# A decoder layer on one NeuronCore: the row transposes and masked sums of the last head groups, made at 32 columns in second PSUM banks

## Chip, cores and metric

The kernel runs on one core of one Trainium2 chip. The metric is device time in microseconds (us) for one launch. Before the change the median of three runs is 803.79 us (803.73 to 803.90).

## What is computed

A pre-LayerNorm decoder layer for 4 sequences of 512 tokens with 512 features and 16 heads of 32, all in fp32:

```python
x = x + self_attention(layernorm(x))        # wq, wk, wv, wo with biases; causal, masked scores -inf
x = x + cross_attention(layernorm(x), ctx)  # q = layernorm(x), k = v = ctx; causal, masked scores -10000
h = layernorm(x)
x = x + relu(h @ Wup.T) @ Wdown.T + sum(softmax(top2(h @ Wgate.T))) * (h @ Wexp)
```

For each head, attention is `softmax(where(causal, q k^T / sqrt(32), masked)) v`. In the cross attention the mask is the finite number -10000, so a masked column still weighs exp(-10000 - row maximum); the kernel carries these weights as a count of the masked columns and a sum of the values behind the diagonal.

## The kernel before

**Stages.** Sequences b = 0 to 3 follow each other. Each has a self attention (its names end in s0 to s3) and a cross attention (c0 to c3), and each attention has two halves. `with_maxima` makes the row maxima of all scores, and mixes in ("fills" with) matmuls of other stages: projections, and the feed-forward network of the sequence before. `attend` makes the scores a second time, exponentiates them and multiplies by the values. Output projection, LayerNorms and feed-forward stand between.

**Groups and units.** The 16 heads form four groups g = 0 to 3 of four heads, whose 4 x 32 features fill 128 partitions. Keys come in four blocks j of 128. `attend` walks ten units n = 0 to 9 of (g, j): (0,0) | (0,3),(0,1) | (0,2),(1,2) | (1,0) | (1,3),(1,1) | (2,0) | (2,3),(2,1) | (2,2),(3,2) | (3,0) | (3,3),(3,1). In each step n it records `scores` of unit n, and from n = 2 on `values` of the unit two before. Scores lie transposed: keys on partitions, queries on columns, two heads in a PSUM pair, so that one unit fills two pairs.

**Row maxima into the scores.** The split (-maximum in three bf16 pieces, `parts[g % 2]`) is transposed by `rows(g)` into PSUM and copied to `mrow[g]`, and a matmul with `onesb` (L416) adds it to the scores before the exponential (L439). So `rows(2)` must be done ahead of unit 5 and `rows(3)` ahead of unit 7. `masked_sums(g)` (L371) is, for cross attention alone, a matmul of `mrow[g]` with a block matrix `same`; `masked(g)` (L377) exponentiates it (`ct_c`) and puts it into the sums.

**Sums of a softmax row.** For the groups in `added` (self 0, 1, 2; cross 0, 2) the exponentials of all key blocks are added up elementwise on DVE (`add_up`, L552) into the tile `sum_` and summed over keys at the end by `summed(g)` (L556-564), a quad of matmuls with a matrix of ones (L558). For other groups the values' matmuls are followed by matmuls with ones (L482). In the self attention `shares` (L466) puts `summed(0)` into the second bank of `pv[1]`, at group 1's first unit, and `summed(1)` into that of `pv[2]`. In the cross attention `summed(g)` goes to the second bank of `pv[g]`. In cross, DVE's `divide`, and POOL's `scale` (L574) follow for the group before. The tile of sums is taken from a pool with one buffer for each tag:

```python
self.sums[g] = act.tile(                     # L428, for units (g, 0) of added groups
    [P, 2, 2, S], F32,
    tag="v" if self.cross else ("ck_t", "beh_t")[g % 2], name=f"sum_{name}")
```

So in the self attention `sum_` of groups 0 and 2 lie in the same buffer.

**PSUM** is one pool `ps` of four buffers, each a pair of banks of 512 fp32 columns (L63-67). Two of them usually go to score pairs, and `pv[g]` holds a pair from its group's first value to its division. Transposes of rows and masked sums take a pair of their own.

**Order.** The instructions of PE, DVE, ACT and POOL stand in the order in which the program is written (`manual_schedule`, L1000; `BY_HAND`, L17). The tile framework adds buffers and the waits between engines. Queued behind a waiting instruction is thus all that is written later for its engine. POOL runs `affine_select` (L447), which sets masked exponentials to zero, and the multiplications of `scale`.

**Around the change, before.** `with_maxima` returns `late`, which says at which step of `attend` rows are made. Its default is {3: 3}: in the self attention both rows(2) and rows(3) are made at n = 3 (one pair `mt_s_both`, eight transposes, two ACT copies); in the cross attention rows(2) is made at the end of `with_maxima`, and rows(3) together with masked_sums(2) at n = 3 (`mt_c_both`). All self stages and c0 to c2 take this path. c3, whose fill has fewer than 20 matmul steps, has {3: 2, 5: 3}. masked_sums(3) of all cross stages is made at n = 7 in a pair of its own (`mb_c`), ahead of that step's values.

Of the kernel before, what the change touches and what calls it, by code (L numbers as in the profile page):

```python
# [18 lines left out]
P = 128  # L19
# [7 lines left out]
def decoder_layer(  # L27
# [21 lines left out]
    nc = tc.nc  # L49
    B, S, D = x.shape  # L50
    NH = 16
    HD = D // NH
    NT = S // P
    NC = D // P
# [10 lines left out]
    def pair(name):  # L65

        return ps.tile([P, 2, S], F32, tag="ps", name=name)
# [198 lines left out]
    class Attention:  # L266
# [82 lines left out]
            nc.vector.tensor_copy(pt[:, :, :, 1], rest)  # L349
            nc.vector.tensor_tensor(pt[:, :, :, 2], rest, pt[:, :, :, 1], ALU.subtract)  # L350

        def rows(self, g, both=None, half=0):


            if both is None:
                tp = ps.tile([P, NT, P], BF16, tag="ps", name=f"mt_{self.name}_{g}")
            else:
                bank = both[:, 0, :].bitcast(BF16)
                tp = bank[:, half * S : (half + 1) * S].rearrange("p (i q) -> p i q", q=P)
            for i in range(NT):  # L360
                nc.tensor.transpose(tp[:, i, :], parts[g % 2][:, i, :], identb)
            self.mrow[g] = work.tile(
                [P, S], BF16, tag="mrow", name=f"mrow_{self.name}_{g}", bufs=4
            )

            def copy(engine=nc.vector.tensor_copy):
                engine(self.mrow[g], tp.rearrange("p i q -> p (i q)"))

            return [copy]

        def masked_sums(self, g, both=None):  # L371

            bc = (pair(f"mb_{self.name}_{g}") if both is None else both)[:, 1, :]
            nc.tensor.matmul(bc, lhsT=same, rhs=self.mrow[g], start=True, stop=True)
            return g, bc

        def masked(self, g, bc):  # L377
# [88 lines left out]
        def shares(self, g, blocks):  # L466

            js = {j for j, *_ in blocks}
            first = js == {0} if g % 2 == 0 else js == {2}
            last = js == {2} if g % 2 == 0 else 1 in js  # L470
            if first:
                self.pv[g] = pair(f"pv_{self.name}_{g}")
            pv = self.pv[g]
            for u in range(1 if g in self.added else 2):
                if u and g == self.joined and (0 in js or 2 in js):
                    if 0 in js:
                        self.joint_sums(pv, blocks[0][2])
                    continue
                for n, (j, c, pts) in enumerate(blocks):
                    for r in range(HG):  # L480
                        h = g * HG + r
                        nc.tensor.matmul(  # L482
                            pv[r * HD : (r + 1) * HD, u, j * P :],
                            lhsT=ones if u else self.v[:, j, h * HD : (h + 1) * HD],
                            rhs=pts[r // 2][:, r % 2, c : c + S - j * P],
                            start=first,
                            stop=last and n == len(blocks) - 1,
                            skip_group_check=True,
                        )
            if self.cross:  # L490


                if (first if g == 1 else js == {0}) and g - 1 in self.added:
                    self.summed(g - 1, self.pv[g - 1])
                    self.divide(g - 1)
                elif js == {0} and g > 0:
                    self.scale(g - 1)
                if 1 in js and g == NC - 1:
                    self.scale(g - 1)
                if last and g not in self.added:  # L500
                    self.divide(g)
                    if g == NC - 1:
                        self.scale(g)
                return
            if first and g == 0:
                self.out = act.tile([P, NC, S], F32, tag="o_t", name=f"oT_{self.name}")
            if (first if g in self.added else js == {0}) and g - 1 in self.added:
                self.sum_in = pv if g in self.added else pair(f"ls_{self.name}")
                self.summed(g - 1, self.sum_in)
            if js == {0} and g - 2 in self.added:  # L510
                self.scale(g - 2)
            if 1 in js and g - 1 in self.added and g not in self.added:
                self.spread(g - 1, self.sum_in)
                self.scale(g - 1)
            if last and g in self.added:
                nc.scalar.copy(self.out[:, g, :], pv[:, 0, :])
                if g > 0:
                    self.spread(g - 1, pv)
            elif last:
                num, den = pv[:, 0, :], pv[:, 1, :]  # L520
                nc.vector.tensor_tensor(
                    self.out[:, g, :], num, self.inverse(g, den), ALU.mult
                )
# [381 lines left out]
    def with_maxima(steps, a, first=0, norms=()):  # L905


        norms = list(norms)
        run(steps[:first])
        fill = matmuls(steps[first:])  # L910
        total = sum(1 if step.__name__ in ("share", "gate") else NC for step in steps[first:])

        units = []
        for g in range(0, NC, 2):
            units += [[(g, 1), (g + 1, 1)]]
            units += [u for k in (g, g + 1) for u in ([(k, 2), (k, 0)], [(k, NT - 1)])]

        lead = 2 if first else 0
        for _ in range(lead):
            next(fill)  # L920
        done, due, jobs, late = lead, float(lead), [], {3: NC - 1}
        todo = []
        for n, pieces in enumerate(units):
            new = a.maxima(pieces)
            if todo:
                todo.pop()(nc.gpsimd)
            if norms and n % 2 == 0:
                new.append(norms.pop(0))
            due += (total - lead) / len(units)

            count = round(due) - done
            for k in range(count):
                next(fill, None)
                done += 1
                if k == min(1, count - 1) and n in (5, 7):
                    jobs = a.rows((n - 5) // 2) + jobs
                if k == min(1, count - 1) and a.cross and n in (6, 8):
                    todo.append(a.masked(*a.masked_sums((n - 6) // 2)))
                if n == len(units) - 1 and k == count - (2 if count > 4 else 1):
                    if total >= 2 * len(units):  # L940
                        if a.cross:
                            a.rows(2)[0](nc.scalar.copy)
                    else:
                        late = {3: 2, 5: NC - 1}
                run(jobs[:1])
                jobs = jobs[1:]
            run(jobs)
            jobs = new
        for _ in fill:
            pass  # L950
        run(jobs)
        return late

    def attend(a, late):


        units = []
# [5 lines left out]
        def values():  # L963
            made = waiting.pop(0)
            a.values(made)

            if len(made) > 1 and made[0][1] == 2:
                held.append(made[1:])
            elif waiting and waiting[0][0][1] > 0:
                if made[0][1] == 0 and held:  # L970
                    a.add_up(held.pop())
                a.add_up(waiting[0] if waiting[0][0][1] == 3 else waiting[0][:1])
                if waiting[0][0][1] == 2 and waiting[0][1][0] == a.joined:
                    a.join(waiting[0][1], waiting[1][0])

        for n, pieces in enumerate(units):
            waiting.append(a.scores(pieces))
            if n in late:
                two = a.cross and late[n] == NC - 1
                together = not a.cross and len(late) == 1  # L980
                both = pair(f"mt_{a.name}_both") if two or together else None
                copies = a.rows(2, both, 1) if together else []
                copies += a.rows(late[n], both)

                more = [a.masked_sums(2, both)] if two else []
                for copy in copies:
                    copy(nc.scalar.copy)
                todo.extend(a.masked(*each) for each in more)
            if a.cross and n == 7:
                todo.append(a.masked(*a.masked_sums(3)))  # L990
            if n in (4 if a.joined is None else 6, 6, 9) and todo:
                todo.pop(0)()
            if n in (3, 4) and put_off:
                put_off.pop(0)()
            if len(waiting) > 2:
                values()
        while waiting:
            values()

# [112 lines left out]
```

## Time and profile before

| | before |
| --- | --- |
| median of the runs | 803.79 us |
| span of the profiled execution | 803.68 us |
| mean granted clock of TensorE (PE) | 0.998 |
| PE busy | 794.0 us, 99% |
| DVE busy | 565.9 us, 70% |
| ACT busy | 395.2 us, 49% |
| POOL busy | 339.6 us, 42% |
| self attention s1, `attend` | 249.9 to 280.1 us of the span |
| cross attention c0, `attend` | 157.4 to 189.2 us of the span |

PE runs matmuls, DVE, ACT and POOL elementwise work. A group of the profile is named by the line of code, the engine, the operation, output and inputs, and its shape. In PE's rows 128\*32 means that 128 rows and 32 columns of the array are used, so that four such matmuls can stand side by side; 32\*128 means that 32 rows are used. "Busy" counts a group from its first to its last matmul, and the ends of matmuls are modelled. An entry such as [0.33 <-PE sc_s L416] says that an engine was idle for 0.33 us in front of this work, and whose end it waited for.

### The profile page before, as it was taken

The numbers are of one execution on the slowest core, as the hardware profiler recorded it, in microseconds if no ns is written. First come the engines' busy times: TensorE is split into PE (matmuls) and PEld (weight loads), VectorE is DVE, ScalarE is ACT, GpSimd is POOL, SyncE is SP. The second block draws the span as 40 slices with busy tenths as digits, with TensorE's granted clock in tenths as the row PEclk, the third lists the DMA queues.
The fourth block names the chain that finished last, engine by engine and source line by source line (L and its number), as shares of the span: only waits on it lengthen the run. The fifth ranks groups of instructions, "written<-read, shape, count | busy, mean of one in ns | idle before, by whom it ended". The sixth has DMA issues, their size and how long they took to land.

```text
span 803.7 us, 13927 instructions
## 1 busy us (share of the span) xinstructions
PE 794.0 (99%) x5588; PEld 378.9 (47%) x5592; DVE 565.9 (70%) x963; ACT 395.2 (49%) x448; POOL 339.6 (42%) x523
## 2 busy tenths in 40 slices
PE   8999999999999999999999999999999999999998
PEld 6444454444444454444544455444444444444544
DVE  2378855889679854678867786588959766988512
ACT  2457516871456615567055742687156833674110
POOL 3434612564234732257332482256423652475100
PEclk9999999999999999999999999999999999999999
DMA  9710000001010000021100000000102000000101
GB/s 301 275 28 1 2 1 1 2 27 54 1 27 2 2 0 1 2 78 55 53 14 14 1 2 0 1 1 2 53 28 80 2 1 1 1 2 1 53 1 52
DMA packets 15282, 24.51 MB, mean 30 GB/s; under 512 B 2033, under 2 KB 5361, under 8 KB 15217
## 3 DMA queue, kind: packets, MB, share of 16 engines
q1 hardware_dynamic: 14496, 22.96, 8.6%
q8 instruction: 44, 0.72, 0.4%
q10 hardware_dynamic: 720, 0.66, 0.2%
q14 instruction: 22, 0.17, 0.1%
HBM read 19.42 MB, written 4.19 MB: 29 GB/s over the span
## 4 chain that ended last, share of the span: by engine, by line
PE 95%; ACT 2%; issue 1%; DMA 1%; DVE 0%; ACTq 0%
PE pm_qk L241 14%; PE pm_d L229 7%; PE pm_u L241 7%; PE pm_v L229 7%; PE pm_o L725 7%; PE pm_e L229 7%; PE pv_c L482 6%; PE pv_s L482 6%; PE sm_c L293 6%; PE sm_s L293 6%; PE sc_s L405 5%; PE sc_c L405 5%; PE sc_s L416 1%; PE sc_c L416 1%; PE tp_a L255 1%
## 5 line engine op out<-in xcount | busy, mean ns | idle before, releaser
L324 DVE TENSOR_REDUCE nm_s<-s_s 128x2 f32<-128x1024 f32 (+3 forms) x128 | 96.9, 810 | 34.7 <-POOL s_s L312 34.7
L324 DVE TENSOR_REDUCE nm_c<-s_c 128x2 f32<-128x1024 f32 (+3 forms) x128 | 95.8, 810 | 31.0 <-POOL s_c L312 31.0
L304 ACT COPY s_s<-sm_s 128x1024 f32<-128x1024 f32 x80 | 77.1, 1015 | 70.7 <-PE sm_s L293 36.7
L304 ACT COPY s_c<-sm_c 128x1024 f32<-128x1024 f32 x80 | 77.1, 1016 | 35.9 <-PE sm_c L293 16.2
L312 POOL TENSOR_SCALAR_AFFINE_SELECT s_c<-s_c 128x512 f32<-128x512 f32 (+1 forms) x80 | 43.9, 550 | 100.4 <-ACT s_c L304 100.4
L312 POOL TENSOR_SCALAR_AFFINE_SELECT s_s<-s_s 128x512 f32<-128x512 f32 (+1 forms) x80 | 43.8, 551 | 94.4 <-ACT s_s L304 94.4
L552 DVE TENSOR_TENSOR sum_s<-sum_s,pt_s 128x256 f32<-128x256 f32 (+2 forms) x72 | 59.9, 897 | 15.4 <-PE pv_s L482 15.4
L439 ACT ACTIVATE pt_c<-sc_c 128x1024 f32<-128x1024 f32 x64 | 61.7, 1031 | 18.1 <-PE sc_c L416 10.1
L447 POOL TENSOR_SCALAR_AFFINE_SELECT pt_c<-pt_c 128x512 f32<-128x512 f32 (+1 forms) x64 | 52.9, 833 | 20.7 <-ACT pt_c L439 20.2
L229 PE MATMUL pm_d<-wdown_sb,hT 128*128 128x512 f32 x128 | 61.5, 611 | 0.0
L241 PE MATMUL pm_qk<-xnT,wk_sb 128*128 128x512 f32 x128 | 61.0, 606 | 0.0
L241 PE MATMUL pm_u<-fT,wup_sb 128*128 128x512 f32 x128 | 59.3, 605 | 0.0
L439 ACT ACTIVATE pt_s<-sc_s 128x1024 f32<-128x1024 f32 x56 | 53.9, 1030 | 10.5 <-POOL pt_s L447 5.5
L229 PE MATMUL pm_v<-wv_sb,xnT 128*128 128x512 f32 x128 | 58.8, 600 | 0.0
L725 PE MATMUL pm_o<-wo_sb,oT_s 128*128 128x512 f32 x128 | 57.8, 596 | 0.0
L405 PE MATMUL sc_c<-cqT,ckT 32*128 32x384 f32 (+3 forms) x512 | 56.4, 464 | 0.9 <-ACT sum_c L439 0.9
L241 PE MATMUL pm_qk<-xnT,wq_sb 128*128 128x512 f32 x120 | 56.7, 605 | 0.0
L229 PE MATMUL pm_e<-wexp_sb,fT 128*128 128x512 f32 x120 | 56.3, 604 | 0.0
L447 POOL TENSOR_SCALAR_AFFINE_SELECT pt_s<-pt_s 128x512 f32<-128x512 f32 (+1 forms) x56 | 48.0, 865 | 16.9 <-ACT pt_s L439 16.2
L405 PE MATMUL sc_s<-qT,kT 32*128 32x128 f32 (+3 forms) x512 | 54.1, 464 | 0.9 <-ACT sum_s L439 0.9
L293 PE MATMUL sm_c<-ckT,cqT 32*128 32x512 f32 (+3 forms) x512 | 47.5, 460 | 0.0
L293 PE MATMUL sm_s<-kT,qT 32*128 32x512 f32 (+3 forms) x512 | 47.0, 461 | 0.0
(171 smaller groups left out, 1268.1 us busy)
## 6 DMA issues: line engine op xcount, KB each, us to landing
cv<-in_ctx_dram SPq DMA_DIRECT2D x16, 256.0 KB, 4.4
out_dram<-x SPq DMA_DIRECT2D x15, 256.0 KB, 2.0
xin<-in_x_dram SPq DMA_DIRECT2D x12, 256.0 KB, 2.8
x<-in_x_dram SPq DMA_DIRECT2D x12, 256.0 KB, 4.2
wq_sb<-in_wq_dram SPq DMA_DIRECT2D x2, 512.0 KB, 6.7
wk_sb<-in_wk_dram SPq DMA_DIRECT2D x2, 512.0 KB, 7.7
wv_sb<-in_wv_dram SPq DMA_DIRECT2D x1, 1024.0 KB, 7.8
wo_sb<-in_wo_dram SPq DMA_DIRECT2D x1, 1024.0 KB, 9.5
```

Source lines behind the costliest of these rows:

```text
L229: nc.tensor.matmul(pm, lhsT=lhs_t[:, c, t * P : (t + 1) * P], rhs=w[:, c, :], start=(c == 0), stop=(c == NC - 1),)
L241: nc.tensor.matmul(pm, lhsT=w[:, c, f * P : (f + 1) * P], rhs=rhs_t[:, c, :], start=(c == 0), stop=(c == NC - 1),)
L293: nc.tensor.matmul(scs[r // 2][:, r % 2, c : c + (i + 1) * P], lhsT=self.q_t[h, g, i * P : (i + 1) * P], rhs=self.k_t[h, g, : (i + 1) * P] ...
L304: nc.scalar.copy(s, scs[n])
L312: nc.gpsimd.affine_select(out=diagonal, in_=diagonal, compare_op=ALU.is_ge, fill=NEG, base=0, pattern=[[0, 2], [0, len(pieces)], [-1, P]], ...
L324: nc.vector.tensor_reduce(self.nm[g][:, i, 2 * n : 2 * n + 2], made[n][:, :, c : c + (i + 1) * P], axis=AX.X, op=ALU.max, negate=True,)
L405: nc.tensor.matmul(scs[r // 2][:, r % 2, c : c + S - j * P], lhsT=self.k_t[h, g, j * P : (j + 1) * P], rhs=self.q_t[h, g, j * P :], start= ...
L439: nc.scalar.activation(pt, scs[n], AF.Exp)
L447: nc.gpsimd.affine_select(out=diagonal, in_=diagonal, compare_op=ALU.is_ge, fill=0.0, base=0, pattern=[[0, 2], [0, len(pieces)], [1, P]], ...
L482: nc.tensor.matmul(pv[r * HD : (r + 1) * HD, u, j * P :], lhsT=ones if u else self.v[:, j, h * HD : (h + 1) * HD], rhs=pts[r // 2][:, r % ...
L552: nc.vector.tensor_tensor(to, to, pts[n][:, :, c : c + S - j * P], ALU.add)
L725: nc.tensor.matmul(pms[t // 2][:, t % 2, :], lhsT=a.out[:, c, t * P : (t + 1) * P], rhs=wo_sb[:, c, :], start=(c == 0), stop=(c == NC - 1),)
```

## The change

`rows` learns a second way (`into`): 16 matmuls with 32 of the columns of `parts` as weights and the identity as the moving side, into the second bank of a given pair. `masked_sums` learns to do its matmul as four of 32 columns. Then these are moved:

- Self attention: rows(2) goes from n = 3 to the end of `with_maxima`, as it was in cross already. rows(3) goes to n = 4, after that step's values, into the second bank of `pv[1]`.
- `summed(0)` of the self attention used that bank from group 1's first unit on. It now comes with unit (1,0), that is with the values of step n = 5, one step later.
- Cross attention c0 to c2: masked_sums(2) stays at n = 3, but after that step's values, as four matmuls in a pair of its own. rows(3) goes to n = 4 into `pv[1]`.
- All cross stages: masked_sums(3) at n = 7 comes after the values and goes to the second bank of `pv[2]`, as four matmuls.
- c3 keeps its rows where they were.

```diff
-        def rows(self, g, both=None, half=0):
-
-
-            if both is None:
+        def rows(self, g, both=None, half=0, into=None):
+
+            if into is not None:
+                tp = into[:, 1, :].rearrange("p (i q) -> p i q", q=P)
+                for i in range(NT):
+                    for r in range(HG):
+                        h = slice(r * HD, (r + 1) * HD)
+                        nc.tensor.matmul(
+                            tp[h, i, :],
+                            lhsT=parts[g % 2][:, i, h],
+                            rhs=identb,
+                            start=True,
+                            stop=True,
+                            skip_group_check=True,
+                        )
+            elif both is None:
...
-            for i in range(NT):
+            for i in range(NT if into is None else 0):
                 nc.tensor.transpose(tp[:, i, :], parts[g % 2][:, i, :], identb)
...
-        def masked_sums(self, g, both=None):
+        def masked_sums(self, g, both=None, columns=False):
 
             bc = (pair(f"mb_{self.name}_{g}") if both is None else both)[:, 1, :]
-            nc.tensor.matmul(bc, lhsT=same, rhs=self.mrow[g], start=True, stop=True)
+            for r in range(HG if columns else 1):
+                h = slice(r * HD, (r + 1) * HD) if columns else slice(0, P)
+                nc.tensor.matmul(
+                    bc[h, :],
+                    lhsT=same[:, h],
+                    rhs=self.mrow[g],
...
-            if (first if g in self.added else js == {0}) and g - 1 in self.added:
+            if js == {0} and g - 1 in self.added:
                 self.sum_in = pv if g in self.added else pair(f"ls_{self.name}")
                 self.summed(g - 1, self.sum_in)
...
-        done, due, jobs, late = lead, float(lead), [], {3: NC - 1}
+        done, due, jobs, late = lead, float(lead), [], True
...
                     if total >= 2 * len(units):
-                        if a.cross:
-                            a.rows(2)[0](nc.scalar.copy)
+                        a.rows(2)[0](nc.scalar.copy)
                     else:
-                        late = {3: 2, 5: NC - 1}
+                        late = False
...
-    def attend(a, late):
+    def attend(a, early):
...
             waiting.append(a.scores(pieces))
-            if n in late:
-                two = a.cross and late[n] == NC - 1
-                together = not a.cross and len(late) == 1
-                both = pair(f"mt_{a.name}_both") if two or together else None
-                copies = a.rows(2, both, 1) if together else []
-                copies += a.rows(late[n], both)
-
-                more = [a.masked_sums(2, both)] if two else []
-                for copy in copies:
-                    copy(nc.scalar.copy)
-                todo.extend(a.masked(*each) for each in more)
-            if a.cross and n == 7:
-                todo.append(a.masked(*a.masked_sums(3)))
+            if not early and n == 3:
+                a.rows(2)[0](nc.scalar.copy)
+            if not early and n == 5:
+                both = pair(f"mt_{a.name}_both")
+                copy = a.rows(NC - 1, both)[0]
+                more = a.masked_sums(2, both)
+                copy(nc.scalar.copy)
+                todo.append(a.masked(*more))
...
             if len(waiting) > 2:
                 values()
+            if early and n == 3 and a.cross:
+                todo.append(a.masked(*a.masked_sums(2, columns=True)))
+            if early and n == 4:
+                a.rows(NC - 1, into=a.pv[1])[0](nc.scalar.copy)
+            if a.cross and n == 7:
+                todo.append(a.masked(*a.masked_sums(3, a.pv[2], columns=True)))
```

More of the change, by code (lines that the diff above doesn't have):

```diff
@@ L369, in rows @@
             return [copy]
-        def masked_sums(self, g, both=None):
+        def masked_sums(self, g, both=None, columns=False):
             bc = (pair(f"mb_{self.name}_{g}") if both is None else both)[:, 1, :]
-            nc.tensor.matmul(bc, lhsT=same, rhs=self.mrow[g], start=True, stop=True)
+            for r in range(HG if columns else 1):
[4 more added lines that the diff above has]
+                    rhs=self.mrow[g],
+                    start=True,
+                    stop=True,
+                    skip_group_check=columns,
+                )
             return g, bc
```

## The prediction

> **What bounds the kernel now.** The page first, for who is busy and whose chain ended last:
>
> ```profile
> PE 794.0 (99%) x5588; PEld 378.9 (47%) x5592; DVE 565.9 (70%) x963; ACT 395.2 (49%) x448; POOL 339.6 (42%) x523
> ...
> PE 95%; ACT 2%; issue 1%; DMA 1%; DVE 0%; ACTq 0%
> ```
>
> PE is busy for 99% of 803.7 us at a granted clock of 0.998, so the end moves by what PE's stream gains or loses. A busy row of PE can hide waits, though: a group is counted from its first to its last matmul. So next come the timelines of the stages that change, here s1 (self attention of sequence 1; the other three differ by hundredths). Columns: start, length, engine, line, work, count. PE:
>
> ```profile
> 257.34 0.62 PE L361 MATMUL mt_s_both<-identb,parts 128*128 128x128 bf16 x8
> 257.89 1.07 PE L482 MATMUL pv_s<-pt_s,v 128*32 128x128 f32 x16
> 258.89 1.50 PE L405 MATMUL sc_s<-qT,kT 32*128 32x128 f32 x16
> 260.53 1.07 PE L482 MATMUL pv_s<-pt_s,v 128*32 128x256 f32 x16
> 261.42 1.16 PE L558 MATMUL pv_s<-sum_s,ones 128*32 128x512 f32 x8
> 262.51 1.14 PE L405 MATMUL sc_s<-qT,kT 32*128 32x512 f32 x8
> 263.80 1.06 PE L482 MATMUL pv_s<-sum_s,v 128*32 128x512 f32 x8
> 264.80 1.31 PE L405 MATMUL sc_s<-qT,kT 32*128 32x128 f32 x16
> ```
>
> and ACT, whose exponentials free the PSUM pairs that the next scores need (in brackets the idle time before, and who ended it):
>
> ```profile
> 253.15 3.78 ACT L439 ACTIVATE pt_s<-sc_s 128x1024 f32<-128x1024 f32 x4
> 257.25 1.94 ACT L439 ACTIVATE sum_s<-sc_s 128x1024 f32<-128x1024 f32 x2 [0.33 <-PE sc_s L416]
> 259.08 1.08 ACT L367 COPY mrow_s<-mt_s_both 128x512 bf16<-128x512 bf16 x2
> 260.50 1.94 ACT L439 ACTIVATE pt_s<-sc_s 128x1024 f32<-128x1024 f32 x2 [0.34 <-PE sc_s L416]
> ...
> 263.89 1.94 ACT L439 ACTIVATE sum_s<-sc_s 128x1024 f32<-128x1024 f32 x2 [0.98 <-PE sc_s L416]
> 266.28 1.94 ACT L439 ACTIVATE pt_s<-sc_s 128x1024 f32<-128x1024 f32 x2 [0.45 <-PE sc_s L416]
> ```
>
> See: at 253-257 ACT runs back to back and paces PE; from n=5 on ACT idles 0.98 and PE paces. Single rows of the trace give the units. One exponential lasts 1.02 us and the next starts 0.92 after it; PE starts 0.05 after an exponential's end; an exponential starts 0.14 after an unstalled score segment's end. A stalled two-piece score segment ends 1.286 after its second pair starts, an unstalled one lasts 1.30. Four 32-column tiles of PE run side by side: a quad of 512-column fp32 matmuls takes 0.853 (L558, two passes of 427 ns). Transposes follow each other by 55 ns, and each change of PE's tiling costs 0.095.
>
> **Self attention, part by part (s1's clock).** (a) rows(2) goes to the end of the maxima pass, where nothing covers it: 4 x 0.055 = +0.22 before the first scores, hence before an exponential chain that paces all up to n=3. (b) The eight transposes at n=3 go: the 0.549 from 257.340 to 257.889. The values then end at 258.34, and n=4's scores, which now lasted 1.643 since their second pair waited, need 1.30 and end at 259.64, 0.89 early (0.549 and a stall of 0.34). (c) What is late next is ACT: exponentials of n=4 at 259.78 and 260.70, the last until 261.72. PE does the values of n=4 (0.95 with the change of tiling) and rows(3): 16 matmuls of 32 columns. Before has no such operation. From below, four side by side at a transpose's spacing: 4 x 0.055 = 0.22. From above, one after another: 16 x 0.055 = 0.88. I take 0.22, since the L482 and L558 quads do run side by side. PE is through at 260.81, but n=5's second pair waits for the exponential ending at 261.72: the stall of 0.9 hides rows(3) at either price. n=5's scores end at 261.77 + 1.29 = 263.05, still 0.75 early. rows(3)'s copy (0.6) sits on ACT behind those exponentials, done by 262.3, before PE wants that pair again.
>
> (d) summed(0), the L558 quads, moves too: it leaves n=4's values for those of n=5. Its work is equal, 2 x 0.427 = 0.853, but sum_s of group 2, which n=5's exponentials write, lies in the one buffer (tag "ck_t") of sum_s of group 0, which summed(0) reads. In the built order of the changed kernel n=5's first exponential accordingly waits for summed(0)'s last matmul; before, that was done ahead of n=5's scores. PE now reaches it after 0.995 of values and 0.853 more: 263.05 + 1.85 = 264.90. The exponential starts at 265.04 rather than 263.89 and ends at 266.06. Queued behind it are ACT's second exponential of n=5 and those of n=6; and n=6's second score pair takes the PSUM pair that it frees. So n=6's scores end at 266.11 + 1.29 = 267.40, against 266.26 before: +1.14. From there n=7's scores and values follow as before, the small stalls shift by a tenth, and n=8 starts 1.0 late (271.6 against 270.58); no idle time of PE is left to take it back up to the last values at 280.11. Everything gained at (b) is inside this.
>
> Self: 0.22 + 1.0 = +1.22 each; in s3, where a 1.02 us copy of the FFN (620.82, hT) stands on ACT just ahead of the first exponential, rows(2)'s copy adds 0.18 and a hundredth or so each side: +1.45. Sum 3 x 1.22 + 1.45 = **+5.1**.
>
> **Cross attention, part by part (c0).** Where PE waits here is at n=8:
>
> ```profile
> 177.67 0.39 PE L374 MATMUL mb_c<-mrow_c,same 128*128 128x512 bf16 x1
> 177.99 1.07 PE L482 MATMUL pv_c<-sum_c,cv 128*32 128x512 f32 x8
> 178.99 1.53 PE L405 MATMUL sc_c<-cqT,ckT 32*128 32x512 f32 x6
> 180.35 0.59 PE L405 MATMUL sc_c<-cqT,ckT 32*128 32x512 f32 x2
> 181.09 1.07 PE L482 MATMUL pv_c<-pt_c,cv 128*32 128x128 f32 x16
> ```
>
> The scores stretch from 178.99 to 181.09, 2.10 for 1.29 of work, since mb_c holds a PSUM pair and their second pair waits for exponentials of n=7. (e) masked_sums(3) into pv[2]'s second bank: the 0.320 (0.213 and a change of tiling) becomes four matmuls of 32 columns inside the values' tiling, between 0.213 (side by side) and 0.853 (serial, 4 x 0.213); I take 0.22. The pair is free, the stall of 0.8 goes, and n=8 ends 0.80 early, n=9's scores 0.65 early. (f) rows(3) at n=4, in c0 to c2: +0.22 against the 0.544 at n=3, which is given back to the exponentials: n=4's end is set by them (168.07 both ways); +0.10 is left through n=7. masked_sums(2) in its new pair costs 0.22 in the room that the 0.544 left. (g) What is late next is POOL:
>
> ```profile
> 180.63 1.97 POOL L574 TENSOR_TENSOR behT<-behT,dt_c 128x512 f32<-128x512 f32 x1
> 182.57 4.04 POOL L447 TENSOR_SCALAR_AFFINE_SELECT pt_c<-pt_c 128x256 f32<-128x256 f32 x4
> ```
>
> The last values need n=8's selects, the second done at 184.52, and they queue behind L574, whose inputs come from DVE and don't move. So the last values end 0.10 early instead of 0.65, and DVE's tail (L552 up to 185.07, then the divisions) 0.12: -0.12 in c0 to c2. c3, with the same order but for (e), -0.2. Sum **-0.56**.
>
> [...] The profile's transposes follow at 55 ns with 128 columns of weights each. [...]
>
> **Sum.** +5.1 - 0.56 = +4.5 on a span of 803.68, which stands 0.11 under the median of 803.79: 808.3.
>
> **Rivals.** *Cross pays in full (B).* L574's start (DVE, 180.63) is one reading of who was last; if the whole 0.65 arrives four times, cross is -2.6 and the sum +2.5: 806.3. For it: PE's 0.8 stall is plainly there. Against: the selects' 184.52. *The moved sums bind nothing (C).* n=5's exponential then starts at 263.19, PE's own work sets n=6: 263.05 + 1.85 + 1.30 = 266.20, about -0.1 by n=8, and with (a) a self stage is +0.12, s3 +0.3. Sum +0.7 - 0.56: 803.9, no difference. Against it stands the one buffer. *The other side (D): PE's stream, not ACT's or POOL's, decides at n=8 of cross.* The mechanism is the second bank: the pair that mb_c kept is free, PE takes 0.65 out of each cross stage. It makes the kernel faster only from the point at which summed(0)'s last matmul comes before 263.2 in s1, so that self keeps its +0.7: then +0.7 - 2.6: 801.9. *32 columns are dear (E):* serial at 0.88, rows(3) costs 0.66 more in three cross stages (self hides it), +2.0: 810.3.
>
> **Chances.** Forecast 0.69 (its own range 807.2 to 809.6: rows(2) up to twice its price, the start-up after summed(0) 0.05 to 0.2), B 0.13, C 0.07, D 0.06, E 0.05. The range from 805.4 to 810.0 takes in the forecast and B and leaves out C, D and E, 0.18. A measurement of this kernel can tell 0.2%, 1.6 us, from no change: D is faster (0.06), C the same (0.07, and 0.01 from B's edge), the rest slower (0.86).
>
> **What would show it.** In s1 of the changed kernel: the exponential of sum_s at n=5 with an idle time near 2 us, ended by PE's row-sum matmuls into pv_s and not by sc_s; n=6's score segment 2.5 us long; n=4's 1.30. If n=5's exponential is released by sc_s, (d) is wrong. In c0: n=8's scores 1.3 long, the last values with a wait on POOL's select; their end more than 0.3 early would mean (g) is wrong. rows(3) longer than 0.3 would show (E).

## The result, and the profile after

The changed kernel takes **808.13 us** (median of 5 runs, 807.92 to 808.91), the kernel before 803.77 us on the same chip: a ratio of **1.0056** (95% interval 1.0043 to 1.0068), slower by about 4.5 us (4.36 between the medians). The forecast was 808.3 us.

The spans of the two profiled executions differ by less, 807.2 against 803.7 us, as they don't start alike: the first row maxima of s0 begin at 26.46 us after and at 27.54 us before, ahead of anything that the change touches. So everything below is compared by stages: from a stage's first maxima to its first scores, and from there to the end of its last values.

| changed kernel against before, us | maxima | scores to last values | both |
| --- | --- | --- | --- |
| s0, s1, s2 | +0.22 | +1.00 | +1.22 |
| s3 | +0.22 | +1.05 | +1.27 |
| c0, c1, c2 | 0.00 | -0.07 | -0.07 |
| c3 | 0.00 | -0.12 | -0.12 |

The sum is +4.6 us: self +4.9, cross -0.3. The page's first part and its chain:

```profile
PE 794.4 (98%) x5697; PEld 379.2 (47%) x5697; DVE 562.8 (70%) x963; ACT 395.7 (49%) x448; POOL 338.0 (42%) x523
...
PE 91%; ACT 4%; DVE 3%; issue 1%; DMA 1%; ACTq 0%; POOL 0%; POOLq 0%
```

PE's busy time is the same to 0.4 us, so the loss is waiting; the chain that ended last, which was PE's for 95% with 2% of ACT and none of DVE, now has 91% of PE, 4% of ACT and 3% of DVE. PE's timeline of s1 (in this execution the first scores of s1 start 0.29 us later than before, 250.23 against 249.94):

```profile
258.63 1.15 PE L426 MATMUL sc_s<-qT,kT 32*128 32x128 f32 x16
259.60 0.40 PE L437 MATMUL sc_s<-mrow_s,onesb 32*128 32x128 bf16 x8
259.93 1.07 PE L503 MATMUL pv_s<-pt_s,v 128*32 128x256 f32 x16
260.81 0.41 PE L359 MATMUL pv_s<-identb,parts 128*32 128x128 bf16 x16
261.15 1.56 PE L426 MATMUL sc_s<-qT,kT 32*128 32x512 f32 x6
...
264.17 1.04 PE L579 MATMUL pv_s<-sum_s,ones 128*32 128x512 f32 x8
265.14 0.49 PE L426 MATMUL sc_s<-qT,kT 32*128 32x128 f32 x4
266.36 1.14 PE L426 MATMUL sc_s<-qT,kT 32*128 32x128 f32 x12 [0.72 <-ACT sum_s L460]
```

Read from start to start: n=4's scores take 1.30 (258.63 to 259.93; 1.64 before). The 16 matmuls of rows(3) (L359) are short. n=5's scores begin early, at 261.15 (262.51 before, on a clock 0.29 us behind this one), and stall. Then n=6's, from 265.14, break in two: 4 matmuls, then a wait for ACT, and the values follow only at 267.64, 2.50 later (1.46 before). ACT says why:

```profile
260.02 1.94 ACT L460 ACTIVATE pt_s<-sc_s 128x1024 f32<-128x1024 f32 x2 [0.54 <-PE sc_s L437]
...
265.28 1.94 ACT L460 ACTIVATE sum_s<-sc_s 128x1024 f32<-128x1024 f32 x2 [2.35 <-PE pv_s L579]
267.66 1.94 ACT L460 ACTIVATE pt_s<-sc_s 128x1024 f32<-128x1024 f32 x2 [0.45 <-PE sc_s L437]
```

The exponentials of n=5, which write `sum_s`, waited 2.35 us and were released not by their scores (sc_s) but by summed(0), L579, whose last matmuls end just ahead of 265.28.

In c0, PE's and then POOL's timeline at the end of the stage:

```profile
178.80 0.40 PE L388 MATMUL pv_c<-mrow_c,same 128*32 128x512 bf16 x4
179.12 1.15 PE L426 MATMUL sc_c<-cqT,ckT 32*128 32x512 f32 x8
...
180.73 1.07 PE L503 MATMUL pv_c<-pt_c,cv 128*32 128x128 f32 x16 [0.24 <-ACT ct_c L402]
...
184.35 1.10 PE L503 MATMUL pv_c<-pt_c,cv 128*32 128x512 f32 x6
185.20 0.60 PE L503 MATMUL pv_c<-pt_c,ones 128*32 128x512 f32 x2
185.27 0.60 PE L503 MATMUL pv_c<-pt_c,cv 128*32 128x512 f32 x2
```

```profile
180.88 1.97 POOL L595 TENSOR_TENSOR behT<-behT,dt_c 128x512 f32<-128x512 f32 x1
182.81 4.04 POOL L468 TENSOR_SCALAR_AFFINE_SELECT pt_c<-pt_c 128x256 f32<-128x256 f32 x4
```

n=8's scores are whole again (the 8 of L426 without a break). The values behind them, which go to `pv[2]`, wait 0.24 for ACT's `ct_c`, which reads masked_sums(3) in that pair's second bank. And the values of unit (3,0), from 184.35, break in pairs: two column tiles (matmuls of 32 columns that run side by side) go on, the other two wait for the select of the second half, which stands behind L595 on POOL, ends at 184.77 in the trace and lets them through at 184.82. The last values take 6.22 us from start to end, 5.73 before.

### The profile page after: what moved, and what is told of

It is laid out like the page before. It is cut to its first block, busy times and chain, and to the rows that moved or that the text cites. A ratio compares the mean times of both kernels' runs of the same rounds, so it can differ in the third digit from the quotient of the medians.

```text
span 807.2 us, 14156 instructions
## 1 busy us (share of the span) xinstructions
PE 794.4 (98%) x5697; PEld 379.2 (47%) x5697; DVE 562.8 (70%) x963; ACT 395.7 (49%) x448; POOL 338.0 (42%) x523
## 4 chain that ended last, share of the span: by engine, by line
PE 91%; ACT 4%; DVE 3%; issue 1%; DMA 1%; ACTq 0%; POOL 0%; POOLq 0%
PE pm_qk L241 13%; PE pm_d L229 7%; PE pm_u L241 7%; PE pm_o L746 7%; PE pm_e L229 7%; PE pm_v L229 6%; PE pv_c L503 6%; PE pv_s L503 6%; PE sm_c L293 6%; PE sm_s L293 5%; PE sc_s L426 5%; PE sc_c L426 4%; PE sc_s L437 1%; DVE nm_s L324 1%; PE sc_c L437 1%
## 5 line engine op out<-in xcount | busy, mean ns | idle before, releaser
L573 DVE TENSOR_TENSOR sum_s<-sum_s,pt_s 128x256 f32<-128x256 f32 (+2 forms) x72 | 56.9, 857 | 13.6 <-PE pv_s L503 13.6
L426 PE MATMUL sc_s<-qT,kT 32*128 32x128 f32 (+3 forms) x512 | 56.9, 463 | 3.7 <-ACT sum_s L460 3.7
L426 PE MATMUL sc_c<-cqT,ckT 32*128 32x384 f32 (+3 forms) x512 | 53.0, 464 | 1.5 <-ACT sum_c L460 0.8
L468 POOL TENSOR_SCALAR_AFFINE_SELECT pt_s<-pt_s 128x512 f32<-128x512 f32 (+1 forms) x56 | 43.3, 782 | 14.5 <-ACT pt_s L460 14.1
```

Source lines behind the costliest of these rows:

```text
L426: nc.tensor.matmul(scs[r // 2][:, r % 2, c : c + S - j * P], lhsT=self.k_t[h, g, j * P : (j + 1) * P], rhs=self.q_t[h, g, j * P :], start= ...
L468: nc.gpsimd.affine_select(out=diagonal, in_=diagonal, compare_op=ALU.is_ge, fill=0.0, base=0, pattern=[[0, 2], [0, len(pieces)], [1, P]], ...
L573: nc.vector.tensor_tensor(to, to, pts[n][:, :, c : c + S - j * P], ALU.add)
```

## The experiments

**Theory:** the one buffer of sums makes n=5's exponentials wait for summed(0) (+1.0 in each self stage), rows(2) has no cover (+0.22), and cross gains little since POOL's multiplication holds the last selects. **Rivals:** the place of summed(0) in PE's own stream, or the 16 matmuls of rows(3), cost the time; and in cross, DVE or the values' order ends the stage. All edits are made to the changed kernel unless it is said otherwise; the code shows the lines that matter. The stage differences in the text are against the kernel before, from the profiles; ratios are to the kernel before on the same chip, with 95% intervals.

**own_sum: the sums of group 2 in another buffer**, in s0 to s2.

```diff
-tag="v" if self.cross else ("ck_t", "beh_t")[g % 2],
+tag="v" if self.cross else
+("ck_t", "beh_t", "ck_t" if self.name == "s3" else "xn_t")[g],
```

> The changed kernel, but in s0 to s2 the sums of group 2 take another buffer (the one of the transposed LayerNorm, idle there); s3 keeps the shared one. Theory (the wait for summed(0) through the one buffer of sums costs each self stage its 1.0 us and the 0.3 us gained before it): n=5's first exponential of s1 is released by the scores and starts about 0.15 after them, n=6's scores are 1.30 long instead of 2.50, the three stages are 1.2 to 1.3 us shorter each and s3 is unchanged: 808.1 - 3.8 = 804.3. Rival 1 (the place of summed(0) in PE's own stream costs, or PSUM pairs do): no change, 808.1, with the stall at another unit. Rival 2 (the 16 matmuls of rows(3) cost): no change, 808.1.

Measured: 805.19 us, ratio 1.0013 (1.0004 to 1.0021). s0 to s2 stand at +0.14 instead of +1.22, s3 at +1.27 as before the edit. ACT and PE in s1:

```profile
261.54 1.94 ACT L461 ACTIVATE sum_s<-sc_s 128x1024 f32<-128x1024 f32 x2 [0.28 <-PE sc_s L437]
```

```profile
263.47 1.15 PE L426 MATMUL sc_s<-qT,kT 32*128 32x128 f32 x16
264.44 0.40 PE L437 MATMUL sc_s<-mrow_s,onesb 32*128 32x128 bf16 x8
264.77 1.07 PE L504 MATMUL pv_s<-pt_s,v 128*32 128x128 f32 x16
```

PE does the same work in the same order, and the exponentials are released by the scores; n=6's scores take 1.30. This settles the buffer against both rivals. The gain of 1.08 for each stage falls short of the 1.2 to 1.3 expected: n=7's scores now take 1.50, with a wait of 0.2 for the exponential of n=6 (1.38 in the changed kernel).

**rows_pv0: summed(0) back in its place at n=4, and rows(3) in the second bank of pv[0]** (self alone).

```diff
-if js == {0} and g - 1 in self.added:
+if (first if g in self.added else js == {0}) and g - 1 in self.added:
...
-a.rows(NC - 1, into=a.pv[1])[0](nc.scalar.copy)
+a.rows(NC - 1, into=a.pv[1 if a.cross else 0])[0](nc.scalar.copy)
```

> The changed kernel, but in the self stages summed(0) stays with group 1's first unit, as before the change, and rows(3) goes to the second bank of pv[0], which nothing else uses there. Theory: summed(0) then falls into PE's stall ahead of n=5's second pair, the exponentials of n=5 need not wait, and each self stage is 1.8 us shorter than in the changed kernel: 808.1 - 7.2 = 801.0 us, which would be below the kernel before. Rival 1 (PE's order): below the changed kernel too, but only by the 1.0 us of each stage: 804. Rival 2 (rows(3) costs): 808.

Measured: 804.33 us, ratio 1.0004 (0.9995 to 1.0012), s0 to s2 at +0.25. The wait is gone here too, but nothing of the time saved at n=3 has come through: the run is 3.3 us short of the expectation. DVE and PE in s1:

```profile
255.06 4.57 DVE L573 TENSOR_TENSOR sum_s<-sum_s,pt_s 128x256 f32<-128x256 f32 x6
263.38 1.52 DVE L573 TENSOR_TENSOR sum_s<-sum_s,pt_s 128x512 f32<-128x512 f32 x2 [3.75 <-PE pv_s L503]
```

```profile
258.02 1.07 PE L503 MATMUL pv_s<-pt_s,v 128*32 128x256 f32 x16
259.08 1.66 PE L579 MATMUL pv_s<-sum_s,ones 128*32 128x512 f32 x8
260.58 0.41 PE L359 MATMUL pv_s<-identb,parts 128*32 128x128 bf16 x16
```

summed(0) reads the sums that DVE adds up, and DVE's six additions end at 255.06 + 4.57 = 259.63; so summed(0) takes 1.66 instead of 1.04. In s0 to s2 of the kernel before it was so already, which the prediction overlooked. Its DVE timeline in s1:

```profile
250.05 1.22 DVE L843 TENSOR_TENSOR x<-pm_d,x 128x1024 f32<-128x1024 f32 x1 [1.25 <-PE pm_d L229]
251.19 1.27 DVE L324 TENSOR_REDUCE nm_s<-s_s 128x2 f32<-128x768 f32 x2
252.38 0.73 DVE L212 TENSOR_SCALAR xn_a<-xin,mv_a,rs_a 128x512 f32<-128x512 f32 x1
253.03 2.33 DVE L324 TENSOR_REDUCE nm_s<-s_s 128x2 f32<-128x1024 f32 x2
...
256.91 4.57 DVE L552 TENSOR_TENSOR sum_s<-sum_s,pt_s 128x256 f32<-128x256 f32 x6
```

DVE has no gap from 250.05 to its last addition at 261.48 (the rows left out follow each other too), and the second half of the first four L558 matmuls starts at 261.53 in the trace. A new theory thus: with summed(0) at n=4, DVE's row of work sets the self stage, and the eight transposes at n=3 cost the kernel before nothing. It holds for s0 to s2. In s3, which has no LayerNorm of a next sequence on DVE, the additions end 0.43 earlier after the first scores, and still the stage stands at +0.30; there rows(3) waits for an ACT copy out of the same pair:

```profile
631.02 0.59 ACT L537 COPY oT_s<-pv_s 128x512 f32<-128x512 f32 x1
631.67 0.41 PE L359 MATMUL pv_s<-identb,parts 128*32 128x128 bf16 x16 [0.28 <-ACT oT_s L537]
```

**cross_only: the self stages as before, the cross stages as after.**

```diff
-if js == {0} and g - 1 in self.added:
+if (first if g in self.added else js == {0}) and g - 1 in self.added:
...
+if early and n == 3 and not a.cross:
+    both = pair(f"mt_{a.name}_both")
+    copies = a.rows(2, both, 1) + a.rows(NC - 1, both)
+    for copy in copies:
+        copy(nc.scalar.copy)
```

(In the full edit rows(2) of self also leaves the maxima, and rows(3) at n=4 is for cross alone.)

> The self stages as before the change, the cross stages as after it. Theory: the parts add, and cross gains the little that its four stages show (0.07 to 0.12 each): 803.8 - 0.35 = 803.4. Rival (the profile hides a gain of the cross stages behind a later one): 801.2.

Measured: 803.61 us, ratio 0.9993 (0.9984 to 1.0002): no difference that can be told. By stages self is 0.00 and cross -0.07, -0.07, -0.08, -0.11. The parts add.

**late_scale: POOL's multiplication of group 1 behind the last selects.**

```diff
                     self.summed(g - 1, self.pv[g - 1])
                     self.divide(g - 1)
-                elif js == {0} and g > 0:
+                    if g == NC - 1:
+                        self.scale(1)
+                elif js == {0} and g == 1:
                     self.scale(g - 1)
```

> The changed kernel, but POOL's multiplication of group 1 in the cross stages comes behind the selects of n=8 and n=9 instead of ahead of them. Theory (in the changed kernel the last values wait for n=8's selects, which queue behind that multiplication): the last values of c0 take 5.73 us again instead of 6.22, each cross stage is 0.5 us shorter up to its last values, of which DVE's divisions after it may take back half: 806.1 to 807.1. Rival (the values' own order, or DVE, holds the end): 808.1, with the last values still 6.2 us long.

Measured: 806.22 us, ratio 1.0030 (1.0018 to 1.0042). Each cross stage is 0.48 to 0.51 shorter than in the changed kernel (-0.55 in c0 to c2 and -0.63 in c3 against before). POOL, then PE, in c0:

```profile
184.40 0.76 POOL L468 TENSOR_SCALAR_AFFINE_SELECT pt_c<-pt_c 128x512 f32<-128x512 f32 x1 [0.28 <-ACT pt_c L460]
185.14 1.71 POOL L597 TENSOR_TENSOR behT<-behT,dt_c 128x512 f32<-128x512 f32 x1
```

```profile
183.57 1.04 PE L503 MATMUL pv_c<-pt_c,cv 128*32 128x512 f32 x8
184.43 1.04 PE L503 MATMUL pv_c<-pt_c,ones 128*32 128x512 f32 x8
```

The values run in full quads again. The gain arrives whole (four stages sum to 1.95, the medians differ by 1.91), so DVE takes nothing back.

**scale_before: the same edit in the kernel before.**

> The kernel before, with POOL's multiplication of group 1 in the cross stages behind the selects of n=8 and n=9, as in late_scale. Theory (before the change PE reached its last values 0.4 to 0.6 us later, owing to the stall of n=8's scores, so POOL held nothing up; only both together are worth something): no change, 803.9. Rival (the multiplication's place is worth 0.5 us in each cross stage by itself): 801.9.

Measured: 804.04 us, ratio 0.9997 (0.9988 to 1.0006), each cross stage 0.00. Taking away PE's stall alone (the changed kernel) is worth 0.07 in c0, moving POOL's multiplication alone nothing, both 0.55: two limits in a row.

**rows3_first: rows_pv0 with rows(3) ahead of summed(0)** (the first edit of rows_pv0 stays, and rows(3) at n=4 is for cross alone).

```diff
+                if g == 1:
+                    self.rows(NC - 1, into=self.pv[0])[0](nc.scalar.copy)
                 self.sum_in = pv if g in self.added else pair(f"ls_{self.name}")
                 self.summed(g - 1, self.sum_in)
```

> As rows_pv0, but rows(3) stands ahead of summed(0) instead of behind it. Theory now (with summed(0) in its old place, the time saved at n=3 turns into a wait of summed(0) for DVE's additions into the sums of group 0, which end 0.6 us after PE's values): the 16 matmuls of rows(3) then lie inside that wait, PE's gap in the values of n=4 falls by 0.2 to 0.3, and each self stage is 0.2 to 0.3 us shorter than in rows_pv0: 804.3 - 1.0 = 803.3. Rival (the gap has another cause, such as the second bank of pv[0] or the order of copies on ACT): no change, 804.3.

Measured: 807.84 us, ratio 1.0039 (1.0026 to 1.0053), s1 at +1.11: a miss of 4.5 us. PE in s1:

```profile
259.16 1.07 PE L503 MATMUL pv_s<-pt_s,v 128*32 128x256 f32 x16
261.73 0.41 PE L359 MATMUL pv_s<-identb,parts 128*32 128x128 bf16 x16 [1.49 <-ACT oT_s L539]
261.95 1.04 PE L581 MATMUL pv_s<-sum_s,ones 128*32 128x512 f32 x8
```

rows(3) goes to the second bank of pv[0], whose first bank ACT copies out (oT_s) behind the exponentials of n=4. In the built program the matmul waits for that copy, though the copy reads the other bank, and summed(0) is queued behind it. In rows_pv0 the same wait lay behind summed(0): in all four self stages rows(3) starts 12.26 us after the first scores, 0.05 after the copy's end. In s0 to s2 DVE's additions hold PE until hundredths before that; in s3 the copy alone holds it, for an estimated 0.44 (the last pass of summed(0) starts at 11.39 and a pass takes 0.43).

**rows3_early: rows(3) written ahead of that copy** (in place of its line in rows3_first).

```diff
             if last and g in self.added:
+                copy = self.rows(NC - 1, into=pv)[0] if g == 0 else None
                 nc.scalar.copy(self.out[:, g, :], pv[:, 0, :])
+                if g == 0:
+                    copy(nc.scalar.copy)
```

> As rows3_first, but rows(3) is written ahead of the copy of group 0's numerators, so that its matmuls need not wait for that copy out of the same PSUM pair. Theory (rows3_first lost 0.86 us in each self stage since rows(3) waited on PE for ACT's copy of pv[0], with summed(0) queued behind it; what then bounds the values of n=4 is the end of DVE's additions): the values of n=4 with rows(3) and summed(0) take 2.6 us (2.90 in rows_pv0, 3.76 in rows3_first), each self stage is 0.2 to 0.3 us shorter than in rows_pv0: 803.3. Rival (the 32-column matmuls in pv[0] disturb the values or the exponentials in another way): 804.3 or more.

Measured: 802.88 us, ratio 0.9981 (0.9972 to 0.9990). The values of n=4 with all that follows them take 2.64 us (2.90 in rows_pv0), and s0 to s2 stand at -0.01, s3 at -0.39. That the first three come back to the time before exactly fits DVE as the bound: in s1 its last addition ends 54.71 us after the first maxima in rows_pv0 and here, 54.72 before the change. rows(2)'s 0.22 lies inside the wait for it in both runs; rows(3)'s 0.23 lies inside it here and behind it in rows_pv0, and that is the +0.25 there. s3, with a shorter row on DVE, gains.

**rows2_pv0: rows(2) at n=2 in the second bank of pv[0]**, in s0 to s3 and c0 to c2.

```diff
-if total >= 2 * len(units):
-    a.rows(2)[0](nc.scalar.copy)
-else:
-    late = False
+late = total >= 2 * len(units)
...
+if early and n == 2:
+    a.rows(2, into=a.pv[0])[0](nc.scalar.copy)
```

> The changed kernel, but rows(2) is made in self s0 to s3 and cross c0 to c2 at n=2, behind that step's values, as 16 matmuls of 32 columns into the second bank of pv[0]. Theory (four transposes at the end of the maxima cost their 0.22 since nothing covers them; at n=2 PE has a stall of 0.6 us behind the exponentials): 0.2 us shorter in each of seven stages, 808.1 - 1.5 = 806.6. Rival (the copy, now in ACT's unbroken row of exponentials, costs 0.46 us in each): 809.8.

Measured: 807.52 us, ratio 1.0034 (1.0021 to 1.0046). The cross stages gain 0.30, 0.17 and 0.30 on the changed kernel; the self stages gain 0.22 in the maxima and lose 0.22 behind it. In s1, ACT and then PE:

```profile
256.77 0.64 ACT L379 CAST mrow_s<-pv_s 128x512 bf16<-128x512 f32 x1
257.55 1.07 PE L503 MATMUL pv_s<-pt_s,v 128*32 128x128 f32 x16
```

The copy falls where ACT waited 0.33 for n=3's scores, and the next exponential starts as in the changed kernel (7.32 us after the first scores against 7.31). But the values of n=3, in the same pair, wait for the copy: they start at 7.61 instead of 7.40, though their scores end alike. The theory held for cross; for self the rival had half its price, by another wait than the one it named.

**best: late_scale, rows2_pv0 and rows3_first together.**

> The cross stages of late_scale, rows(2) as in rows2_pv0 and rows(3) as in rows3_first. Theory: the parts add, -1.0 of rows3_first and -1.5 of rows2_pv0 and -1.9 of late_scale on the 804.3 of rows_pv0: 799.9, below both kernels. Rival (ACT's chain, with a copy more, or DVE's additions take the place of what is saved): 802 or more.

Measured: 805.11 us, ratio 1.0005 (0.9996 to 1.0014). Self at +1.10 carries the wait of rows3_first; cross at -0.85, -0.72, -0.85, -0.65 is as summed. The parts add; one of them was wrong.

**cross_best: the self stages as before, with the cross stages of late_scale and rows2_pv0 together.**

> The self stages as before the change; the cross stages as after it, with POOL's multiplication of group 1 behind the last selects and rows(2) at n=2 in the second bank of pv[0]. Theory (stages add): -0.85, -0.72, -0.85 and -0.65 us in c0 to c3, 803.9 - 3.1 = 800.8. Rival (what the cross stages gain is taken back by what follows): above 802.

Measured: 801.80 us, ratio 0.9970 (0.9958 to 0.9982); the stages sum to -3.0 us, the interval is -3.4 to -1.4.

**best2: these cross stages; in self, rows3_early, and rows(2) at n=3 behind the values.**

```diff
+if early and n == (2 if a.cross else 3):
+    a.rows(2, into=a.pv[0])[0](nc.scalar.copy)
```

> The cross stages of cross_best; in the self stages rows(2) at n=3 behind the values and rows(3) as in rows3_early, both in the second bank of pv[0], and summed(0) in its place of before. Theory (rows(2) then lies in the time that PE waits for DVE's additions at n=4 and its copy in an idle time of ACT): each self stage 0.2 to 0.3 us shorter than before the change, 800.8 - 1.0 = 799.8. Rival (the copy of rows(2) holds up the values of n=4, which write to the same pair): 801 or more.

Measured: 799.93 us, ratio 0.9949 (0.9937 to 0.9962). The time is as expected, the reason isn't: s0 to s2 stand at +0.02 and not at -0.2 to -0.3; s3 at -0.51. The stages sum to -3.5. rows(2) left the maxima and saved 0.22 there, and the values of n=4 lost it again, waiting for DVE, whose additions start 6.97 us after the first scores as before the change.

**late_norm: best2 with 0.66 us less in DVE's row.** The last LayerNorm piece of the next sequence (L212) goes to n=5, where DVE idles.

```diff
+later.extend([norms.pop()] if more else [])
 late = with_maxima(between_self, sa, skip, norms)
...
+if n == 5 and later:
+    later.pop()()
```

> best2, but in s0 to s2 the last LayerNorm piece of the next sequence (0.66 us of DVE) stands at n=5, where DVE idles, instead of between the last row maxima. Theory (in the self stages DVE works without a gap from the end of the maxima to its last addition into the sums of group 0, and summed(0), so every kernel that keeps summed(0) at n=4 ends the self stage at the same time, whatever PE saves at n=3): the values of n=4 with rows(3) and summed(0) take 2.0 to 2.1 us instead of 2.66, s0 to s2 are 0.5 to 0.65 us shorter each, s3 is as before: 799.9 - 1.8 = 798.1. Rival (ACT's exponentials or the copy of rows(2) hold n=4): no change, 799.9.

Measured: **798.78 us**, ratio 0.9928 (0.9915 to 0.9941). DVE, then PE, in s1:

```profile
253.02 5.02 DVE L578 TENSOR_TENSOR sum_s<-sum_s,pt_s 128x256 f32<-128x256 f32 x6
257.96 0.54 DVE L212 TENSOR_SCALAR xn_a<-xin,mv_a,rs_a 128x512 f32<-128x512 f32 x1
```

```profile
256.88 0.64 PE L503 MATMUL pv_s<-pt_s,v 128*32 128x256 f32 x8
...
258.00 1.15 PE L584 MATMUL pv_s<-sum_s,ones 128*32 128x512 f32 x8
259.07 0.71 PE L426 MATMUL sc_s<-qT,kT 32*128 32x512 f32 x4
```

summed(0) takes 1.15, and n=4's values 2.19 (256.88 to 259.07) instead of 2.66. s0 to s2 are 0.47 shorter than in best2, s3 is unchanged to the hundredth. One instruction moved off DVE's row shortens a stage that PE's count shows as 99% busy: DVE was the bound there. DVE's additions start 6.05 us after the first scores instead of 6.97, but take 5.02 instead of 4.57 (the third of the six 1.38 instead of 0.95), for a cause that no run takes apart; so 0.47 of the 0.92 comes through, and the last addition, which ends at 258.04, still sets the second half of summed(0).

## Why the prediction was right, and where it wasn't

- **(a) rows(2) without cover:** +0.22 in all four stages, as worked out.
- **(b) the transposes and n=4's stall:** n=4's scores took 1.30 as forecast and ended 0.89 early. What the prediction missed, and the total didn't show, is the bound beside it: DVE's additions ended at 261.48 and let the second half of the L558 matmuls through at 261.53. With summed(0) at n=4 the 0.89 brings nothing forward; it can only cover rows(2) and rows(3) (rows3_early at -0.01). The values of n=4 before, 1.978 with summed(0), held 0.1 us of that wait, which the prediction passed over. It did not touch the sum only because the change moves summed(0) away from it; that is luck.
- **(c) rows(3):** 0.23 (values with it 1.225, 0.996 without) against 0.22 taken; E falls. Its copy ended at 262.64 in the clock of before, not by 262.3, as ACT's copy of the numerators (L537, 0.59) stands ahead of it; the pair's next values start at 263.00, so that cost nothing. The Trainium skill, "TensorE: Matmul & The Clock Gate", LDWEIGHTS (loading the stationary operand), puts a load in ns at its columns over 1.2, from which sixteen loads of 32 columns, one after another, are an estimate of 16 x 27 ns = 0.43 us. That is not what the trace shows, and the measurement decides.
- **(d) the buffer of sums:** the exponential at 264.99 in the clock of before (265.28 less 0.29), forecast 265.04; n=6's scores 2.50, forecast 2.5; n=8 at 271.59, forecast 271.6. own_sum shows the mechanism. C had the price right for a kernel without that wait (+0.12 a stage, measured +0.14), but not the kernel.
- **s3:** forecast +1.45, measured +1.27. The FFN's copy (hT) ahead of rows(2)'s cost nothing, not 0.18. ACT after, then before:

```profile
623.15 1.02 ACT L811 ACTIVATE hT<-pm_u 128x1024 f32<-128x1024 f32 x1
624.07 0.58 ACT L379 COPY mrow_s<-mt_s 128x512 bf16<-128x512 bf16 x1
624.65 1.94 ACT L460 ACTIVATE sum_s<-sc_s 128x1024 f32<-128x1024 f32 x2
```

```profile
620.82 1.02 ACT L790 ACTIVATE hT<-pm_u 128x1024 f32<-128x1024 f32 x1
622.09 1.94 ACT L439 ACTIVATE sum_s<-sc_s 128x1024 f32<-128x1024 f32 x2 [0.25 <-PE sc_s L416]
```

rows(2)'s transposes put off the first scores by 0.22 but not hT, which now starts 0.12 ahead of them instead of 0.11 behind. So rows(2)'s copy fits in front of the first exponential, which starts 1.38 after the first scores in both. The 0.05 by which s3 still loses more than the others lies in the kernel before: from first scores to last values s3 took 30.19 and s1 30.24 there, and 31.24 and 31.25 after.

- **(e), (f), (g) cross:** -0.07 each and -0.12 in c3, forecast -0.12 and -0.2. The limit on POOL was right and is shown by late_scale and scale_before; B falls. The sizes were off. n=8's scores end 0.8 early as forecast, but (e) took `pv[2]` for free: the values behind them wait for ACT's `ct_c` (179.89 to 180.58) in its second bank and start 0.51 early. n=9's scores then end 0.55 early, not 0.65, and the last values take 0.49 longer (6.22 against 5.73), so that 0.07 is left. No run takes the wait for `ct_c` away; it stands at 0.24 in best2 too. The sum of cross is -0.34 against -0.56.
- **D** would have needed both limits gone, POOL's and the buffer's. Each is taken away in a run of its own: own_sum leaves +0.14 in a self stage, late_scale -0.55 and -0.63 in a cross stage. An estimate from these, 4 x 0.14 - 3 x 0.55 - 0.63 = -1.7 us, comes near D's 801.9, but no run has both. DVE's bound is no part of it, as summed(0) stays late there.

The two errors of size, 0.18 too much in s3 and 0.22 too much gain in cross, cancel, and so the total is closer than its terms; that too is luck.

Left open: why one of DVE's additions is longer in late_norm. A version with summed(0) late, its own buffer in all four stages and the lighter DVE row was not run.

## What to carry to other kernels

When the last reader of a one-buffer tile is moved to a later step, look for who writes that buffer next: the wait appears on another engine than the one whose work was moved, and with hand-written order all that is queued there waits too. Before counting a freed piece of the busiest engine as gained, follow each of its next inputs back to the engine that makes it; an engine busy for 70% of the span can have no gap in the one stretch that counts. And a second bank is not free by itself: where the program is built to wait by the pair, what is written there waits for readers of the first bank (rows3_first), and what is written to the first bank for readers of the second (rows2_pv0, and `ct_c` in the cross stages). Two limits that stand close behind each other are worth nothing one at a time (0.07 and 0.00) and something together (0.55).

## What the runs showed of the hardware

Column tiles of one PE quad can fall out of step, and then stay so: in c0 of the changed kernel the second pair of tiles waits until 184.82 in the trace while the first makes its second pass at 184.78, after which the quads run as two pairs some 60 to 70 ns apart, one quad's second pair beside the next quad's first. The whole group takes 0.49 us longer (6.22 against 5.73): the pair that did not wait saved nothing by going ahead. Weights of 32 columns were loaded in rows of 97 ns (median), those of 128 columns in the transposes in 98 ns, and neither showed in the spacing of the matmuls (four of 32 columns every 56 ns, a transpose every 55 ns).
